# Two residual blocks on one Trainium2 core: the second layer's input finished by an accumulating DMA and ScalarE

## The chip, the cores and the metric

The kernel runs on one core of one Trainium2 chip. The core has a matrix engine (PE, TensorE), a vector engine (DVE, VectorE), an activation engine (ACT, ScalarE), a general engine (POOL, GpSimd) and a queue that mostly issues DMAs (SP, SyncE). They run at the same time and wait for one another by semaphores; each takes its own instructions in order. The metric is the device time of one execution in microseconds: 2819.61 us before the change, the median of three runs (2818.54 to 2820.89).

## The reference, cut to what matters

The input is 64 images of 1024 channels of 14 x 14, in float32. Two bottleneck layers follow one another.

```python
# layer 0: 1x1 to 256, 3x3, 1x1 to 1024; batch statistics over all 64 images
out = relu(_bn(_conv(x, w1, b1), g1, be1))
out = relu(_bn(_conv(out, w2, b2, pad=1), g2, be2))
out = _bn(_conv(out, w3, b3), g3, be3)
y = relu(x + softplus(residual_scale) * out)
# layer 1: deformable; statistics per image and group of channels
a = relu(group_norm(conv(y, w1), ...))
om = conv(a, w_off, pad=1) + b_off          # 27 maps: 9 x offsets, 9 y offsets, 9 masks
sampled = bilinear_sample(a, py, px) * sigmoid(mask)
h2 = relu(group_norm(einsum("bckhw,ock->bohw", sampled, w2), ...))
out = relu(group_norm(conv(h2, w3), ...) + y)
```

Because layer 0's last norm needs statistics over all images, the raw result of its third convolution is written to memory (`h3`) and finished later: `y = relu(scale * h3 + shift + x)`. That last step is what the change is about.

## The kernel before, in words

Two images make a pair, and there are 32 pairs. A pair's activations are tiles of 128 partitions (channels) by 8 blocks by 392 columns (2 x 196 positions).

Layer 0 runs as three loops over all pairs. Products of 2 x 2 blocks are formed with seven instead of eight matmuls, so sums stand before and after the matmuls on DVE, ACT and POOL. Its second convolution leaves even and odd image columns in separate planes. The third convolution (L732 to L863; matmuls at L735, L770, L836) keeps that order in PSUM (`planes`) and stores it to `h3`, one pair after the other. `x` of pairs 0 to 2 is loaded into three of four `Y` buffers during this loop.

Layer 1 runs as one software pipeline over pairs. Pass t, for t from 2 to 29, is written out by hand in `steady(t)` (L1933 to L1974): it lists small steps for PE, and puts steps for the other engines between them at numbered places. On PE, ACT, DVE and POOL the order of the list is the order of the queue. SP's order is left to a planner, except where an instruction is marked to keep its program order. Passes 0, 1, 30 and 31 are made by `slot(t)`, where only PE's order is by hand. In pass t the order on PE is:

- `d1`: the first convolution of pair t+1 (L1109), which reads `y` of pair t+1 (`q["y"]`, one of the four `Y` buffers).
- `sp[0]` woven with the first half of the third convolution `d3` of pair t-1. `sp` samples pair t (L1430, copied out of PSUM by ACT, L1438). In `d3` (L1679), four groups of seven matmuls each need `E` (ACT, L1683), then `V` (DVE, L1686), two sums on POOL (L1691) and two on DVE (L1695, L1699).
- the offset convolution of pair t+1 (`om`, L1205). At its end ACT and DVE form an even and an odd sum (L1220 to L1222), and then six small DVE sums write the offsets (`off`, L1232).
- `sp[1]` woven with the rest of `d3`; at place 7 `selection(t+1)`: ACT's mask (L1244), stores to `dm`, loads of `wt` and `mk`; and there also `load(t+2)`: SP loads `x` into the `Y` buffer (L196) and `h3` into the buffer `Z0` (L204).
- `pd[0]` and `pd[1]`: the second convolution of pair t (L1542), with transposes of pair t+1, the bilinear weights of pair t+1 (`distances`, `end`; L1271 to L1291), the third norm of pair t-1 (a pow on POOL, L1054; scaling on ACT, L1762), and at place 21 of `pd[0]` `residual(t+2)`. In `pd[1]` ACT copies `E` (L1566), DVE forms `V` (L1572), and POOL two sums (L1573, L1574). `output(t-1, 0)` adds `y` (L1778), applies ReLU (L1780) and stores `z` (L1783).

`residual(p)` finishes layer 0 for pair p: for each of the 8 blocks, DVE computes `y = h3 * scale + x`, which also turns the planes of `h3` into image order (L216), and ACT applies shift and ReLU (L228).

Of the kernel before, what the change touches and what calls it, by code (L numbers as in the profile page):

```python
# [16 lines left out]
P = 128  # L17
H = W = 14
HW = H * W
# [25 lines left out]
def kernel(  # L45
# [163 lines left out]
    def end_of_first(p, r, b):  # L209


        def natural(v):
            return v.rearrange("p (r x b) -> p r x b", x=7, b=2)

        y = natural(Y[p % 4][:, b, :])
        return nc.vector.scalar_tensor_tensor(  # L216
            y,

            r[:, b, :].rearrange("p (b r x) -> p r x b", x=7, b=2),
            bn3.sc[:, b : b + 1],  # L220
            y,
            ALU.mult,
            ALU.add,
        )
# [430 lines left out]
    with l0, tc.manual_schedule(  # L655
# [19 lines left out]
        def planes(t):  # L675
            return t.rearrange("p (b n) -> p b n", b=2)

        def relu(p, c, n):
            v = inputs(p, c, n)
            nc.scalar.activation(  # L680
                v, v, AF.Relu, bias=bn2.sh[:, c : c + 1], scale=bn2.sc[:, c : c + 1]
            )
# [49 lines left out]
        for p in range(2):  # L732
            pts = [ps.tile([P, N2], FP, tag=f"ps{o % 4}", name=f"c3_{p}_{o}") for o in range(CB)]
            for o, c in [(o, c) for c in range(MB) for o in range(CB)]:
                nc.tensor.matmul(  # L735
                    planes(pts[o]),
                    w3_sb[:, c, ts(o, P)],
                    inputs(p, c),
                    start=(c == 0),
                    stop=(c == MB - 1),  # L740
                )
            if p == 0:
                for c in range(MB):
                    relu(2, c, 2)
                Ts = input_sums(2)
            else:
                weight_sum(3)
            for o in range(CB):
                d = place(p, o)
                if o % 2:  # L750
                    nc.vector.tensor_scalar(d, pts[o], bias(o), None, ALU.add)
                else:
                    nc.scalar.activation(d, pts[o], AF.Identity, bias=bias(o))
                waiting.append((o, p, d))
                statistics()
            for jj in range(2):
                store_h3(p, jj)
# [5 lines left out]
        for p in range(2, NP - 2, 2):  # L763
            tt = Ts
            for j in range(HB):
                acc = [ps.tile([P, N2], FP, tag=f"ps{m}", name=f"c3_{p}_{j}_{m}") for m in range(4)]
                part = ts(j, P)

                def product(m, a, b, start):
                    nc.tensor.matmul(  # L770
                        planes(acc[m]), a, b, start=start, stop=True, skip_group_check=True
                    )

                e1, e5, e7, u2, w = (
                    ep.tile([P, N2], FP, tag=v, name=f"{v}_{p}_{j}")
                    for v in ("e1", "e5", "e7", "u2", "w")
                )
                (c11, c12), (c21, c22) = ([place(p + i, o) for i in range(2)] for o in (j, HB + j))
                product(0, a11[:, part], inputs(p, 0), True)
                nc.scalar.copy(e1, acc[0])  # L780
                product(1, S[1][:, part], tt[1], True)
                nc.scalar.copy(e5, acc[1])
                product(2, S[3][:, part], tt[3], True)
                nc.scalar.activation(e7, acc[2], AF.Identity, bias=bias(HB + j))
                nc.gpsimd.tensor_tensor(w, e5, e7, ALU.add)
                product(3, S[2][:, part], tt[2], True)

                statistics()
                nc.vector.tensor_tensor(u2, acc[3], e1, ALU.add)
                nc.gpsimd.tensor_tensor(c22, w, u2, ALU.add)  # L790

                product(0, a12[:, part], inputs(p, 1), False)
                nc.scalar.activation(c11, acc[0], AF.Identity, bias=bias(j))
                product(1, S[4][:, part], inputs(p + 1, 1), False)
                nc.vector.scalar_tensor_tensor(c12, acc[1], bias(j), u2, ALU.add, ALU.add)
                product(2, a22[:, part], tt[4], False)
                nc.vector.scalar_tensor_tensor(c21, acc[2], bias(HB + j), u2, ALU.add, ALU.add)
                waiting += [(j, p, c11), (j, p + 1, c12), (HB + j, p, c21), (HB + j, p + 1, c22)]
                if j < 2:
                    relu(p + 2, j, 2)  # L800
                if j == 1 and p in folded:
                    bn3.fold(folded[p], p)
                if j == 2 and p + 2 < NP - 2:
                    Ts = input_sums(p + 2)
                elif j == 2:
                    Ds = [differences(p + 2 + i) for i in range(2)]
                if j % 2:
                    for i in range(2):
                        store_h3(p + i, j // 2)
            if p in (6, 10, 14):  # L810
                load_x((p - 6) // 4)
            elif p == 22:
                load_h3(0, Z0)
            elif p == 26:
                load_h3(1, Z1)

                nc.scalar.activation(small.tile([P, 1], FP, tag="sp_a", name="table"), rs, AF.Sigmoid)
# [8 lines left out]
        for p in range(NP - 2, NP):  # L826
            for o in range(CB):
# [5 lines left out]
                    else ((S[1][:, j], inputs(p, 0)), (a22[:, j], Ds[p - NP + 2]))  # L833
                )
                for m, (a, b) in enumerate(ab):
                    nc.tensor.matmul(planes(pt), a, b, start=(m == 0), stop=(m == 1))  # L836
                d = place(p, o)
                statistics()
                nc.scalar.activation(d, pt, AF.Identity, bias=bias(o))
# [85 lines left out]
    def build_second_bottleneck(l1, path, run, early):  # L925
# [159 lines left out]

        def load(p):
            start(p)

            load_x(p, tc.keep_in_program_order)
            load_h3(p, Z0, tc.keep_in_program_order)  # L1090

        def residual(p, b0=0, b1=CB):

# [93 lines left out]
        def offset_conv(p):  # L1187
# [3 lines left out]
            def step(n):  # L1191
# [20 lines left out]
                if n == 3 * MB - 1:  # L1212


                    om = one.tile([P, N2], FP, tag="om", name=f"om_{p}")[:32]
                    m1, m0, m2, m3 = (
                        q["po"][ts(m, 32)].rearrange("p i q -> p (i q)") for m in range(4)
                    )
                    even, odd = om[:, :HW], om[:, HW:]
                    nc.scalar.activation(even, m1, AF.Identity, bias=boff_sb[:32])  # L1220
                    nc.vector.tensor_tensor(odd, even, m2, ALU.subtract)
                    nc.vector.tensor_tensor(even, even, m2, ALU.add)  # L1222

                    q["om"] = one.tile([32, N2], FP, tag="off", name=f"off_{p}")
                    for h0, h1, _ in groups:
                        dst = q["om"][:, cols(h0, h1)].rearrange("p (i q n) -> p i q n", i=2, n=2)
                        for n, (a, b, op) in enumerate(((even, m0, ALU.add), (odd, m3, ALU.subtract))):
                            a, b = (
                                v.rearrange("p (i q) -> p i q", i=2)[:, :, h0 * half : h1 * half]
                                for v in (a, b)  # L1230
                            )
                            nc.vector.tensor_tensor(dst[:, :, :, n], a, b, op)  # L1232

            return [lambda n=n: step(n) for n in range(3 * MB)]

        def selection(p):

# [1 line left out]

            def step():  # L1240

                om = q["om"]
                mask = one.tile([P, N2], FP, tag="om", name=f"mask_{p}")[:32]
                nc.scalar.activation(mask, om, AF.Sigmoid)  # L1244
# [592 lines left out]
        def slot(t):  # L1837
# [59 lines left out]
            if back and t == NP - 1:  # L1897
                extra.append((32, lambda: output(t - 1, 0)))
            extra += [(20, lambda: first_sum(t, 1))] if this and E == 2 else []
            extra += [(21, lambda: residual(t + 2))] if more else []  # L1900
            extra = [(scale(k), s) for k, s in extra]
            extra.sort(key=lambda v: v[0])
            todo += put(pd[0], [s for _, s in extra], [k for k, _ in extra])
# [12 lines left out]
                extra += list(zip((5, 5, 11), first_norm(2)))  # L1916
            if bare:
                extra.append((n - 6, lambda: corners(t + 1, 0)))
            if back and t < NP - 1:
                extra.append((n * 18 // 28, lambda: output(t - 1, 0)))  # L1920
            elif back:
# [11 lines left out]
        def steady(t):  # L1933
# [9 lines left out]
            def at(steps, *extra):  # L1943
# [5 lines left out]
                ((0,), [lambda: scaled(t - 2, 1)]),  # L1949
                ((1, 1, 7, 9, 9, 10, 10, 10), norm2),  # L1950
                ((6,), [lambda: output(t - 2, 1)]),
                ((10,), [lambda: corners(t, 0)]),
            )
            todo += at(weave(sp[0], d3[:half]), ((4, 4, 8, 14, 16, 18, 21), norm1))
# [1 line left out]
            todo += offset_conv(t + 1)  # L1956
            todo += at(
                weave(sp[1], d3[half + 2 :]),
                ((7, 7), selection(t + 1) + [lambda: load(t + 2)]),
            )  # L1960
            todo += at(
                pd[0],
# [1 line left out]
                ((5, 20), [lambda e=e: first_sum(t, e) for e in range(2)]),  # L1964
                ((6, 11, 16, 21), transposes(t + 1)),
                ((6, 13), [distances, end]),
                ((21,), [lambda: residual(t + 2)]),
            )
            todo += [lambda: list(spread_rows(t + 1, 0)), lambda: list(spread_columns(t + 1, 0))]
            todo += [lambda: list(spread_rows(t + 1, 1)), lambda: lend(t + 1)]  # L1970
            todo += at(pd[1], ((16,), [lambda: output(t - 1, 0)]))
            todo.append(lambda: list(spread_columns(t + 1, 1)))
            for step in todo:
                step()  # L1974
# [200 lines left out]
```

## Time and profile before

| what | value |
|---|---|
| median of the runs | 2819.61 us (2818.54 to 2820.89) |
| the profiled execution | 2822.43 us |
| its span, first to last instruction | 2820.6 us |
| mean granted clock of PE | 0.991 |
| busy in a pass of 56.3 us: PE, DVE, ACT, POOL | 56.14, 48.2, 34.0, 14.4 us |
| DMA, mean over the span | 150 GB/s |

The profile is of one execution, taken by the hardware profiler. Times are in us from the start of the span. A row of the timeline has a start, a duration, the engine, the line, the operation, the tile written and the tiles read, the shape and a count. In square brackets stands how long the engine had been idle before it and what released it. PE shows each float32 matmul as two records. A table by stretches gives each engine's busy time in a part of the span, then the granted clock as a fraction, the mean busy share of the 16 DMA engines, and the GB/s that they moved. Instructions that only issue a DMA do not count as busy.

### The profile page before, as it was taken

How to read it: one execution, taken by the hardware profiler on the slowest of the kernel's cores; microseconds unless marked ns; L12 is line 12 of the kernel's file. 1: busy time of each engine (PE TensorE's matmuls, PEld its weight loads, DVE VectorE, ACT ScalarE, POOL GpSimd, SP SyncE). 2: the span in 40 equal slices, each digit the busy share in tenths (PEclk: the TensorE clock that was granted, in tenths of full speed). 3: DMA queues.
4: the chain of work that ended last, by engine and by line, in shares of the span. 5: the costliest groups of instructions: out<-in, count | busy, mean ns of one | idle time of the engine just before them, and what ended most of it. 6: DMA issues, size and time to landing. Idle time of an engine off the chain costs nothing.

```text
span 2820.6 us, 39474 instructions
## 1 busy us (share of the span) xinstructions
PE 2756.8 (98%) x12930; PEld 2013.2 (71%) x12930; DVE 2376.8 (84%) x4900; ACT 1341.3 (48%) x2723; POOL 951.5 (34%) x1069
## 2 busy tenths in 40 slices
PE   9999899998999989999999999999999999999997
PEld 5555555554555567887888788878887888788874
DVE  7877899998788778888888888888888888888876
ACT  0000221212555545566556655665566556655654
POOL 4630366664666302222222222222222222222221
PEclk9999999999999999999999999999999999999998
DMA  8656000003656444555455545554555455545541
GB/s 233 193 172 175 23 1 0 1 1 132 222 190 227 169 132 146 181 173 189 147 183 175 189 142 182 179 183 146 183 174 190 142 188 172 190 139 190 170 134 58
DMA packets 350315, 424.19 MB, mean 150 GB/s; under 512 B 27892, under 2 KB 292500, under 8 KB 349844
## 3 DMA queue, kind: packets, MB, share of 16 engines
q1 hardware_dynamic: 350100, 421.57, 45.7%
q8 instruction: 104, 1.70, 0.3%
q14 instruction: 111, 0.91, 0.1%
HBM read 296.49 MB, written 116.76 MB: 147 GB/s over the span
## 4 chain that ended last, share of the span: by engine, by line
PE 59%; DVE 2%; issue 1%; DMA 1%; ACT 0%; POOL 0%; SPq 0%; DVEq 0%; ACTq 0%; POOLq 0%
PE pd L1542 22%; PE sp L1430 12%; PE d L1109 11%; PE d L1679 10%; PE om L1205 2%; PE tr L1308 1%; DVE V L1686 1%; PE pd L1461 1%; DMA X<-wd 1%; DMA S<-wd 1%; DVE st L1005 0%; SPq L1393 0%; DVE z L1793 0%; SPq L1349 0%; PE d L1728 0%
## 5 line engine op out<-in xcount | busy, mean ns | idle before, releaser
L1430 PE MATMUL sp<-S,aT 126*128 126x420 f32 (+3 forms) x1536 | 488.3, 416 | 9.1 <-DVE S L1410 7.3
L1438 ACT COPY sm<-sp 128x336 f32<-128x336 f32 (+3 forms) x640 | 288.9, 452 | 257.9 <-PE sp L1430 217.0
L1542 PE MATMUL pd<-sm,w2b_sb 128*128 128x196 f32 x2232 | 400.7, 329 | 0.0
L1542 PEld LDWEIGHTS pd<-sm,w2b_sb 128*128 128x128 f32 x2232 | 371.3, 190 | 0.0
L534 PE MATMUL c<-v,u_sb 128*128 128x392 f32 x1024 | 342.9, 497 | 11.0 <-DVE bn1sh L167 8.2
L1109 PE MATMUL d<-h,w1b_sb 128*128 128x392 f32 x1024 | 345.3, 495 | 2.8 <-ACT h L228 2.8
L534 PEld LDWEIGHTS c<-v,u_sb 128*128 128x128 f32 x1024 | 194.5, 191 | 159.3 <-issue 11.7
L1542 PE MATMUL pd<-sm,Sc 128*128 128x196 f32 x1674 | 308.0, 329 | 0.0
L1109 PEld LDWEIGHTS d<-h,w1b_sb 128*128 128x128 f32 x1024 | 194.0, 191 | 139.5 <-ACT h L228 6.4
L1498 DVE TENSOR_TENSOR sm<-sm 128x980 f32<-128x980 f32 (+2 forms) x257 | 265.8, 1053 | 16.8 <-PE pd L1542 10.1
L1542 PEld LDWEIGHTS pd<-sm,Sc 128*128 128x128 f32 x1674 | 278.7, 190 | 0.2
L1430 PEld LDWEIGHTS sp<-S,aT 126*128 126x128 f32 x1536 | 259.3, 191 | 22.3 <-issue 10.7
L1762 ACT ACTIVATE z<-z,gn_0sh,gn_0sc 128x196 f32<-128x196 f32 x496 | 225.2, 537 | 18.0 <-DVE gn_0sh L1077 18.0
L520 DVE TENSOR_TENSOR v<-t 128x392 f32<-128x392 f32 x256 | 193.0, 812 | 0.0
L1573 POOL TENSOR_TENSOR E<-V,E 128x196 f32<-128x196 f32 x31 | 18.6, 599 | 516.7 <-DVE V L1572 516.7
L1679 PE MATMUL d<-h,w3b_sb 128*128 128x196 f32 x744 | 174.0, 329 | 0.8 <-ACT h L1594 0.8
L1679 PEld LDWEIGHTS d<-h,w3b_sb 128*128 128x128 f32 x744 | 133.6, 189 | 51.6 <-issue 19.1
L1691 POOL TENSOR_TENSOR E<-V,E 128x196 f32<-128x196 f32 x124 | 74.3, 599 | 282.6 <-DVE V L1686 282.6
L1410 DVE TENSOR_TENSOR S<-S,X 126x840 f32<-126x840 f32 (+1 forms) x192 | 159.4, 882 | 11.8 <-DMA X<-wd 10.7
L1780 ACT ACTIVATE z<-z 128x784 f32<-128x784 f32 x124 | 105.8, 857 | 104.3 <-DVE z L1778 102.6
L389 PE MATMUL c<-xc,w1a_sb 128*128 128x392 f32 x384 | 149.1, 497 | 5.6 <-DMA xc<-in_x_dram 5.6
L216 DVE SCALAR_TENSOR_TENSOR h<-h,bn3sc,h 128x392 f32<-128x392 f32 x256 | 140.9, 622 | 0.0
(690 smaller groups left out, 4975.0 us busy)
## 6 DMA issues: line engine op xcount, KB each, us to landing
xc<-in_x_dram SPq DMA_DIRECT2D x128, 392.0 KB
h<-o SPq DMA_DIRECT2D x64, 784.0 KB
h<-in_x_dram SPq DMA_DIRECT2D x64, 784.0 KB
h<-h SPq DMA_DIRECT2D x64, 784.0 KB
out_dram<-z SPq DMA_DIRECT2D x124, 392.0 KB
X<-wd SPq DMA_DIRECT2D x64, 413.4 KB
S<-wd SPq DMA_DIRECT2D x64, 413.4 KB
S<-wd SPq DMA_DIRECT2D x64, 330.8 KB
```

Source lines behind the costliest of these rows:

```text
L216: return nc.vector.scalar_tensor_tensor(y,  r[:, b, :].rearrange("p (b r x) -> p r x b", x=7, b=2), bn3.sc[:, b : b + 1], y, ALU.mult, ALU ...
L389: nc.tensor.matmul(acc[m], a, b, start=(j == 0), stop=(j == HB - 1))
L520: nc.vector.tensor_tensor(v[:, u].rearrange("p (i y x) -> p i y x", y=7, x=7), cols[c][:, :, i : i + 13 : 2, :], cols[c][:, :, j : j + 13 ...
L534: nc.tensor.matmul(m[u], u_sb[:, c, u, k % 4, ts(o, P)], vts[k][c][:, u], start=(c == 0), stop=(c == MB - 1),)
L1109: nc.tensor.matmul(q["pt"][o], w1b_sb[:, c, ts(o, P)], q["y"][:, c, :], start=(c == 0), stop=(c == CB - 1),)
L1410: nc.vector.tensor_tensor(S[:, piece], S[:, piece], X(piece), ALU.mult)
L1430: nc.tensor.matmul(pt[:, i], q["aT"][:, i0 + i, c, starts.index(r0), :], q["S"][e][g, r0][:, :, i0 + i, :], start=(j == 0), stop=(j == len ...
L1438: nc.scalar.copy(dst, pt.rearrange("p i k n -> p k i n"))
L1498: return nc.vector.tensor_tensor(dst, a, b, ALU.subtract)
L1542: nc.tensor.matmul(bank[:, m % 2], a[:, k], b[:, k - k0],  start=(k == 0 and m in (5, 0, 2, 6)), stop=(k == T - 1), skip_group_check=True,)
L1679: nc.tensor.matmul(bank[:, m % 2 if m < 6 else 1], a, b, start=(m < 6), stop=True, skip_group_check=True)
L1762: nc.scalar.activation(z[:, ts(i, HW)], z[:, ts(i, HW)], AF.Identity, bias=n.sh[:, b, i : i + 1], scale=n.sc[:, b, i : i + 1],)
```

## The change

Four things change together.

1. Layer 0's third convolution writes its PSUM tiles in image order (`columns` in place of `planes`: neighbouring outputs lie two words apart within a plane), so `h3` is in image order, and `end_of_first` no longer reorders.
2. In layer 1 `load(p)` loads `h3` straight into the `Y` buffer and no `x`. In `steady` it moves from place 7 of `sp[1]` to place 7 of `d1`.
3. `residual` in the loop is replaced by three steps: `first_scaled` (eight ACT instructions, scale and shift, at place 0 of `pd[0]`), `add_x` (two DMAs issued by POOL that add `x` from memory onto `Y`, at place 12 of `pd[0]`), and `first_relu` (four ACT instructions of two blocks each, at place 0 of `pd[1]`). `slot` gets the same steps at similar places. `residual` remains for pair 2 in the filling of the pipeline.
4. The six offset sums leave the end of `offset_conv` for a step of their own, `offsets`, at place 4 of `sp[1]`, behind the `V` of the running group of `d3`.

```diff
     def end_of_first(p, r, b):
-        def natural(v):
-            return v.rearrange("p (r x b) -> p r x b", x=7, b=2)
-
-        y = natural(Y[p % 4][:, b, :])
+        y = Y[p % 4][:, b, :]
         return nc.vector.scalar_tensor_tensor(
             y,
-            r[:, b, :].rearrange("p (b r x) -> p r x b", x=7, b=2),
+            r[:, b, :],
             bn3.sc[:, b : b + 1],
             y,
             ALU.mult,
             ALU.add,
         )
...
+        def columns(t):
+            return t.rearrange("p (n b) -> p b n", b=2)
...
                 nc.tensor.matmul(
-                    planes(pts[o]),
+                    columns(pts[o]),
...
                     nc.tensor.matmul(
-                        planes(acc[m]), a, b, start=start, stop=True, skip_group_check=True
+                        columns(acc[m]), a, b, start=start, stop=True, skip_group_check=True
...
-                    nc.tensor.matmul(planes(pt), a, b, start=(m == 0), stop=(m == 1))
+                    nc.tensor.matmul(columns(pt), a, b, start=(m == 0), stop=(m == 1))
...
         def load(p):
             start(p)
-            load_x(p, tc.keep_in_program_order)
-            load_h3(p, Z0, tc.keep_in_program_order)
+            load_h3(p, Y[p % 4], tc.keep_in_program_order)
+
+        def first_scaled(p):
+            for b in range(CB):
+                y = Y[p % 4][:, b, :]
+                nc.scalar.activation(
+                    y, y, AF.Identity, bias=bn3.sh[:, b : b + 1], scale=bn3.sc[:, b : b + 1]
+                )
+
+        def add_x(p):
+            for i in range(2):
+                nc.gpsimd.dma_start(
+                    Y[p % 4][:, :, ts(i, HW)],
+                    x[2 * p + i].rearrange("(b p) q -> p b q", p=P),
+                    accum_op=ALU.add,
+                )
+
+        def first_relu(p):
+            for b in range(0, CB, 2):
+                y = Y[p % 4][:, ds(b, 2)]
+                nc.scalar.activation(y, y, AF.Relu)
...
                     om = one.tile([P, N2], FP, tag="om", name=f"om_{p}")[:32]
...
+                    q["sums"] = om[:, :HW], om[:, HW:]
+                    even, odd = q["sums"]
+                    m1, m2 = (q["po"][ts(m, 32)].rearrange("p i q -> p (i q)") for m in (0, 2))
                     nc.scalar.activation(even, m1, AF.Identity, bias=boff_sb[:32])
                     nc.vector.tensor_tensor(odd, even, m2, ALU.subtract)
                     nc.vector.tensor_tensor(even, even, m2, ALU.add)
-                    q["om"] = one.tile([32, N2], FP, tag="off", name=f"off_{p}")
-                    for h0, h1, _ in groups:
...
+        def offsets(p):
+            q = pairs[p]
+            half = W // 2
+            (even, odd), (m0, m3) = q["sums"], (q["po"][ts(m, 32)] for m in (1, 3))
+            q["om"] = one.tile([32, N2], FP, tag="off", name=f"off_{p}")
+            for h0, h1, _ in groups:
+                dst = q["om"][:, cols(h0, h1)].rearrange("p (i q n) -> p i q n", i=2, n=2)
+                for n, (a, b, op) in enumerate(((even, m0, ALU.add), (odd, m3, ALU.subtract))):
+                    a = a.rearrange("p (i q) -> p i q", i=2)
+                    a, b = (v[:, :, h0 * half : h1 * half] for v in (a, b))
+                    nc.vector.tensor_tensor(dst[:, :, :, n], a, b, op)
...
         def selection(p):
             def step():
+                if "om" not in q:
+                    offsets(p)
...
-            extra += [(21, lambda: residual(t + 2))] if more else []
+            extra += [(2, lambda: first_scaled(t + 2)), (12, lambda: add_x(t + 2))] if more else []
...
+            if more:
+                extra.append((n * 8 // 28, lambda: first_relu(t + 2)))
...
                 ((6,), [lambda: output(t - 2, 1)]),
+                ((7,), [lambda: load(t + 2)]),
                 ((10,), [lambda: corners(t, 0)]),
...
                 weave(sp[1], d3[half + 2 :]),
-                ((7, 7), selection(t + 1) + [lambda: load(t + 2)]),
+                ((4, 7), [lambda: offsets(t + 1)] + selection(t + 1)),
...
-                ((21,), [lambda: residual(t + 2)]),
+                ((0, 12), [lambda: first_scaled(t + 2), lambda: add_x(t + 2)]),
...
-            todo += at(pd[1], ((16,), [lambda: output(t - 1, 0)]))
+            todo += at(pd[1], ((0,), [lambda: first_relu(t + 2)]), ((16,), [lambda: output(t - 1, 0)]))
```

More of the change, by code (lines that the diff above doesn't have):

```diff
@@ L1215, in step @@
                     om = one.tile([P, N2], FP, tag="om", name=f"om_{p}")[:32]
[L1216 to L1219, printed above, removed]
+                    q["sums"] = om[:, :HW], om[:, HW:]
+                    even, odd = q["sums"]
+                    m1, m2 = (q["po"][ts(m, 32)].rearrange("p i q -> p (i q)") for m in (0, 2))
                     nc.scalar.activation(even, m1, AF.Identity, bias=boff_sb[:32])
@@ L1222, in step @@
                     nc.vector.tensor_tensor(even, even, m2, ALU.add)
-                    q["om"] = one.tile([32, N2], FP, tag="off", name=f"off_{p}")
-                    for h0, h1, _ in groups:
[L1226 to L1232, printed above, removed]
-            return [lambda n=n: step(n) for n in range(3 * MB)]
+            return [lambda n=n: step(n) for n in range(3 * MB)]
+        def offsets(p):
[9 more added lines that the diff above has]
+                    nc.vector.tensor_tensor(dst[:, :, :, n], a, b, op)
         def selection(p):
```

## The prediction

> **What bounds the kernel.** I read the page first: PE is busy for 98% of the span, DVE for 84%, ACT for 48%. A share of the span is a mean over stages, so next I read busy time in stretches of 56.3 us, the length of one pass of the second layer's loop.
>
> ```profile
> PE 2756.8 (98%) x12930; PEld 2013.2 (71%) x12930; DVE 2376.8 (84%) x4900; ACT 1341.3 (48%) x2723; POOL 951.5 (34%) x1069
> ```
>
> ```profile
> 1771.80:1828.20 56.40, 56.24 (x320) 46.37 (x319) 48.30 (x107) 34.08 (x72) 14.42 (x19) 1.00 0.53 176
> 1828.20:1884.50 56.30, 56.14 (x320) 46.27 (x319) 48.21 (x107) 33.99 (x72) 14.41 (x19) 1.00 0.50 166
> ```
>
> The columns are length, then busy us (and counts) of PE, PEld, DVE, ACT and POOL, then granted clock, DMA share and GB/s. PE is idle for 0.16 us of a pass. All 28 such stretches look alike and make 1577 us of the 2820.6. DVE has 8 us to spare in each. So taking work off DVE is worth nothing here unless a PE wait hangs on it. The timeline of PE in one pass shows the one wait:
>
> ```profile
> 1805.58 0.73 PE L1430 MATMUL sp<-S,aT 126*128 126x336 f32 x2
> 1806.47 0.60 PE L1679 MATMUL d<-T,w3b_sb 128*128 128x196 f32 x2 [0.16 <-DVE V L1686]
> ```
>
> Start to start is 0.89 us, where the same pair without a wait takes 0.57 us (1804.68 to 1805.25): a stall of 0.32 us. DVE's timeline says why: V stands behind the six offset sums.
>
> ```profile
> 1804.43 1.38 DVE L1232 TENSOR_TENSOR off<-om,om 32x84 f32<-32x84 f32 x6
> 1805.85 0.57 DVE L1686 TENSOR_TENSOR V<-d,E 128x392 f32<-128x392 f32 x1
> ...
> 1823.12 4.40 DVE L216 SCALAR_TENSOR_TENSOR h<-h,bn3sc,h 128x392 f32<-128x392 f32 x8
> ```
>
> **Offset sums behind V.** V could start at 1804.43 and end at 1805.0. PE's matmul would then issue at 1806.15, as it would with no wait. The offset sums end 0.57 us later, which delays the mask, the two stores to dm and the loads of wt and mk. Their first reader, L1271 at 1816.76, has some 5 us over, and the loads that followed them on SP's queue are gone from there. Worth 28 x 0.32 = 9.0 us.
>
> **DVE's residual removed.** 8 x 0.55 = 4.40 us per pair leave DVE, worth nothing at a PE without waits.
>
> **ScalarE's new work.** Eight scalings with scale and bias pointers replace nothing at the start of `pd[0]`, T0 = 1812.40 here. L228 (one pointer, 392 wide) costs 4.22 us for eight; L1762 (two pointers, 196 wide) shows 0.08 us more of fixed cost each, so I take 0.61 us x 8 = 5.0 us: from 1812.7, after the last sm copy, to 1817.7. ACT has the room:
>
> ```profile
> 1814.80 0.37 ACT L1311 COPY aT<-tr 126x256 f32<-126x256 f32 x1 [2.10 <-PE tr L1308]
> 1817.76 0.86 ACT L1272 ACTIVATE wt<-wt 126x784 f32<-126x784 f32 x1 [2.58 <-DVE wt L1271]
> ...
> 1824.03 4.22 ACT L228 ACTIVATE h<-h,bn3sh 128x392 f32<-128x392 f32 x8
> 1830.45 0.49 ACT L1566 COPY E<-pd 128x392 f32<-128x392 f32 x1 [2.20 <-PE pd L1542]
> ```
>
> The aT copy slips by 2.9 us (its PSUM buffer is wanted again only by the fourth transpose at 1820.02) and Abs by 0.3 us (the next DVE step runs at 1820.67 anyway). Four ReLUs of 784 at 0.87 us (row L1780, 0.86) then stand where L228 stood: 3.5 us for 4.2. Without lateness this costs nothing; with the cover gone it would be 5.0 us a pair.
>
> **The load moved.** Two h3 loads (L204, 784 KB each) go from behind the selection to step 7 of `d1`, two x loads (L196) leave SP. On SP they follow the spreads of X and the stores of z at 1785.6, and SP has nothing behind them until 1805.8. They wait for the z+y sum that ends at 1784.1. They stand behind the stores in one queue, so do not slow them. At the 350 to 410 GB/s of the loads below they need 4.3 us, and land by 1799; the reader comes at 1812.7. Nothing.
>
> **The accumulating DMA** is what decides. It sits on POOL behind the pow of 1815.84 to 1817.4, waits for the last scaling (1817.7), and moves 2 x 802,816 B in rows of 784 B. Behind it on POOL stand the E and h2 sums at 1833.76, 16 us later. The ReLUs wait for it; behind these on ACT stands E (L1566), behind E comes V (L1572 at 1833.12), then h2, its norm, and PE's third convolution; and the first convolution, at 1834.17, reads the ReLUs' output. Where is the deadline? If both transfers land at time L, E ends at L + 4.0 instead of 1830.94. V then starts at L + 4.0 instead of 1833.12, and in the next pass the T sums on POOL are ready some 2 us ahead of the matmuls that read them (1787.41 against 1789.42). So L up to about 1831.2 is free, and each us later costs one us of PE. The first convolution's own limit is 1834.17 - 0.9 = 1833.3, less strict.
>
> When does it land? The DMA engines, in the same pass (share and GB/s are the last columns):
>
> ```profile
> 1814.00:1816.00 2.00, 2.00 (x15) 1.98 (x14) 1.79 (x8) 0.37 (x1) 0.16 (x1) 1.00 1.11 353
> 1816.00:1818.00 2.00, 2.00 (x15) 1.97 (x14) 2.00 (x3) 0.24 (x1) 1.40 (x1) 1.00 1.11 400
> 1822.00:1824.00 2.00, 2.00 (x14) 2.00 (x13) 2.00 (x4) 2.00 (x7) 0.00 (x0) 1.00 0.36 99
> 1826.00:1828.00 2.00, 2.00 (x14) 2.00 (x13) 2.00 (x4) 2.00 (x5) 0.00 (x0) 1.00 0.53 186
> 1830.00:1832.00 2.00, 2.00 (x14) 2.00 (x13) 2.00 (x3) 1.20 (x2) 0.00 (x0) 1.00 0.57 224
> 1832.00:1834.00 2.00, 2.00 (x14) 2.00 (x13) 0.99 (x3) 1.97 (x5) 0.24 (x1) 1.00 0.70 228
> ```
>
> A plain pair load runs at about 378 GB/s with the engines full: 1.61 MB in 4.25 us. No row shows an accumulate. Its bounds: once that price, and three times or more. The Trainium skill, DMA: Bandwidth & Descriptors, section Anatomy of one DMA, fits a POOL-issued DMA as 2.0 us plus bytes over 436 GB/s. By it both are down 5.7 us after 1817.7, at 1823.4: in time. The same page's Rules for kernel authors speak against that: an accumulate reads its destination before it writes it. Two streams read for one written make 8.5 us of full engines, an estimate from the page and the row. I take this, since the plain rate is already that of full engines. From 1819 (1.3 us to begin, an estimate from the page's first-byte figure), some 0.7 of the engines is free until 1822 (the stores of wd alone, estimated) and 0.64 and 0.74 in the next two stretches: 4.9 us of engine time by 1826; of the other 3.6 us half-shares bring the end to 1833.2, and leftovers alone to 1835.5. With 1 us to complete, L is 1834.2 to 1836.5: 3.0 to 5.3 us late. I take 3.6, nearer the even share.
>
> A second rule, SBUF — State Buffer, section SBUF: two separate sides, says that DVE in a two-port mode keeps POOL from writing descriptors. In 1817.7 to 1821 DVE runs almost only tensor_tensor, which by the same page has no such mode. Followed blindly it would add the DVE rows in that stretch, 3 us a pair (87 us); I add nothing.
>
> **First layer in image order.** Matmul outputs go to PSUM at a step of two words (L735, L770, L836: 64 + 784 + 64 records of 0.329 us pitch, 300 us). No row shows a strided PE write: between 0 and +300 us, and I take 0, since a column already takes 0.84 ns. The 16 residual instructions of the first two pairs lose their stride: at most 16 x 0.06 = 1 us. Taken as 0.
>
> **Sum.** The profiled execution took 2822.4 us (span 2820.6). Minus 9.0, plus 29 pairs (3 to 31) x 3.6 = 104: 2917.8. The median of the runs is 2.8 us below the profiled time: 2915.
>
> **The rivals.** *In time, faster:* the accumulate costs less than about 1.6 plain loads (6.8 us of engines), L stays under 1831.2, ACT never blocks, only the 9.0 us remain: 2811 (2803 to 2816). For it: the pass's DMA share of 0.53 and the page's fit. Against: the second read. *Far late:* at three prices or with slow descriptors on POOL, 12.8 us of engines end near 1843: 13 us x 29 = 377 us, about 3190. The stores of z then slip too: they drain by about 1793, just when POOL rewrites z (1793.47). And stalls of 3 us or more lower the clock:
>
> ```profile
> 1018.00:1020.00 2.00, 0.38 (x4) 0.17 (x2) 0.00 (x0) 0.00 (x0) 0.00 (x0) 1.00 0.58 219
> 1020.00:1022.00 2.00, 0.66 (x1) 0.50 (x2) 1.80 (x4) 0.25 (x1) 0.00 (x0) 0.64 0.59 217
> 1022.00:1024.00 2.00, 2.00 (x4) 0.94 (x3) 2.00 (x6) 1.34 (x4) 0.00 (x0) 0.50 0.60 232
> ```
>
> After 3 us of idle PE runs at half clock for 5.4 us, 2.7 us lost; 29 times would be 78 us. *Strided writes slow:* up to 3100 alone.
>
> **Chances.** A few us late 0.42 (own range 2850 to 2985); in time 0.31; far late 0.22; strided writes or another cause 0.05. A measurement tells some 0.2% (5.6 us) from no change: of the in-time case 0.04 falls within it, and 0.03 of the late case where lateness just eats the 9 us. So faster 0.27, same 0.07, slower 0.66. The range must hold the in-time case below and stops where 0.17 of far late and strided writes is left above, at 2.35 plain prices (7 us a pair, with some lost clock): 2804 to 3045.
>
> **What would show it.** V's wait gone and L1686 ahead of the offset sums: the 9 us right. ACT idle before the 784-wide ReLUs, released by a DMA later than 19 us after T0, and PE idle before L1109 or L1679: the late case, with the idle time as its size. No such idle, and a pass of 56.0 us: in time. Longer L770 durations: the strided write. I would be wrong if the accumulate runs at the plain rate, or if it runs with so little overlap that a row at a time pays its full latency.

## The result: 2888 us, 2.4% slower

The changed kernel takes 2888.36 us (median of four runs, 2886.1 to 2889.72) where the kernel before takes 2820.23 in the same session: a ratio of 1.0242 [1.0224, 1.0259]. The profiled execution has a span of 2884.0 us against 2820.6, at a granted clock of 0.992.

First the page of the changed kernel: busy time, the two large DMA queues (packets, MB, share of 16 engines' span), the chain that ended last, and the adding DMA (KB each, median us from issue to landing).

```profile
PE 2782.8 (96%) x12930; PEld 2015.4 (70%) x12930; DVE 2254.8 (78%) x4668; ACT 1428.9 (50%) x2839; POOL 1044.8 (36%) x1127
...
q1 hardware_dynamic: 289780, 375.01, 40.8%
q0 software_dynamic: 60320, 46.57, 11.5%
...
PE 32%; DMA 14%; DVE 7%; ACT 7%; issue 3%; SPq 2%; POOL 1%; DVEq 0%; ACTq 0%; POOLq 0%
...
h<-in_x_dram POOLq DMA_DIRECT2D x58, 784.0 KB, 10.6
```

The same chain of the kernel before:

```profile
PE 59%; DVE 2%; issue 1%; DMA 1%; ACT 0%; POOL 0%; SPq 0%; DVEq 0%; ACTq 0%; POOLq 0%
```

DVE lost 122 us of work, about as forecast, and PE still lost time. The chain was 59% PE before; now a DMA holds 14% of it. The queue q0 carries only the adding DMAs: 46.57 MB in 60320 packets, 772 B each. Its 11.5% of 2884.0 us are 332 us, or 11.4 us over 16 engines for each of 29 pairs. (It is a sum of packet times. Stretches below add up to more than 1, so it isn't an occupancy; it serves to compare kernels.) Two stretches of one pass's length show where PE stands (columns as in the prediction):

```profile
1861.50:1920.00 58.50, 57.29 (x320) 46.51 (x319) 44.05 (x98) 37.28 (x77) 17.61 (x21) 1.00 0.65 167
1920.00:1978.50 58.50, 57.33 (x320) 46.44 (x320) 44.08 (x99) 37.36 (x77) 17.64 (x21) 1.00 0.63 167
```

The same 320 matmuls need 58.5 us. PE is idle for 1.2 of them instead of 0.16; its busy time is 1.2 us longer too, since a pair of matmuls behind a wait is longer in the records (0.60 us for L1702 in the timeline below, 0.50 without a wait). So idle time alone shows half of the loss. I measure passes from the start of one offset convolution to that of the next: 56.33 us before, 58.41 after, mean of 27 passes.

The chain of waits (us in all, times, longest us; PEld is PE's weight load):

```profile
ACT h L1109 <- DMA h<-in_x_dram: 250.8, 29, 9.7
...
DVE V L1595 <- ACT E L1589: 137.2, 29, 7.0
...
PEld d L1702 <- ACT h L1617: 40.8, 31, 4.1
PEld sp L1453 <- DVE S L1433: 26.4, 30, 2.3
PEld d L1702 <- DVE z L1718: 20.0, 30, 1.0
...
PE d L1702 <- ACT h L1617: 21.6, 30, 3.5
...
PE sp L1453 <- DVE S L1433: 19.0, 31, 2.0
```

Read down, it is one path: the ReLUs wait for the adding DMA, `V` for `E` behind the ReLUs, PE's third convolution for the second norm's ReLU (L1617), its sampling matmuls for `S`, a product on DVE, and later in the pass the third convolution's weight loads for DVE's sum `z` (L1718). The timeline of one pass, with T0 = 1896.40, has the places (rows of DVE, ACT, POOL, PE and SP put together in order of time):

```profile
1888.77 0.57 DVE L1709 TENSOR_TENSOR V<-d,E 128x392 f32<-128x392 f32 x1
1889.36 1.38 DVE L1255 TENSOR_TENSOR off<-om,om 32x84 f32<-32x84 f32 x6
...
1896.60 4.95 ACT L1094 ACTIVATE h<-h,bn3sh,bn3sc 128x392 f32<-128x392 f32 x8
1901.91 3.19 POOL L1100 DMA_DIRECT2D h<-in_x_dram  x2 [0.50 <-ACT aT L1334]
1903.54 4.26 SPq L1314 DMA_DIRECT2D wd<-wt  x4
1913.67 2.44 SPq L1372 DMA_DIRECT2D S<-wd  x3
1916.80 3.10 ACT L1109 ACTIVATE h<-h 128x784 f32<-128x784 f32 x4 [8.66 <-DMA h<-in_x_dram]
1919.81 0.46 ACT L1589 COPY E<-pd 128x392 f32<-128x392 f32 x1
1920.30 0.57 DVE L1595 TENSOR_TENSOR V<-pd,E 128x392 f32<-128x392 f32 x1 [4.48 <-ACT E L1589]
1929.41 0.60 PE L1702 MATMUL d<-h,w3b_sb 128*128 128x196 f32 x2 [0.54 <-ACT h L1617]
1930.51 0.97 PE L1453 MATMUL sp<-S,aT 126*128 126x420 f32 x2 [0.49 <-DVE S L1433]
```

The first two rows are the offset sums behind `V`: that part does what it says. The ReLUs start at T0+20.4, ACT having stood for 8.66 us, and `V` at T0+23.9 where it was at T0+20.72: 3.18 us late. The first convolution, which begins at T0+21.78 in both kernels, isn't held up. PE pays after it, at the third convolution. The engines' share during the adding DMAs (last two columns):

```profile
1904.00:1906.00 2.00, 2.00 (x15) 1.98 (x14) 2.00 (x3) 2.00 (x6) 1.11 (x1) 1.00 0.97 111
1906.00:1908.00 2.00, 2.00 (x14) 2.00 (x13) 1.21 (x2) 2.00 (x7) 0.00 (x0) 1.00 1.23 201
1908.00:1910.00 2.00, 2.00 (x14) 2.00 (x13) 0.00 (x0) 0.14 (x1) 0.00 (x0) 1.00 1.27 181
1914.00:1916.00 2.00, 2.00 (x14) 2.00 (x13) 1.82 (x3) 0.00 (x0) 0.00 (x0) 1.00 1.02 162
```

Full engines, at half the GB/s that the plain loads of before reached with full engines (353 and 400).

### The profile page after: what moved, and what is told of

The parts are those of the page before. It is cut to its first block, busy times and chain, and to the rows that moved or that the text cites. A ratio compares the mean times of both kernels' runs of the same rounds, so it can differ in the third digit from the quotient of the medians.

```text
span 2884.0 us, 39588 instructions
## 1 busy us (share of the span) xinstructions
PE 2782.8 (96%) x12930; PEld 2015.4 (70%) x12930; DVE 2254.8 (78%) x4668; ACT 1428.9 (50%) x2839; POOL 1044.8 (36%) x1127
## 3 DMA queue, kind: packets, MB, share of 16 engines
q0 software_dynamic: 60320, 46.57, 11.5%
## 4 chain that ended last, share of the span: by engine, by line
PE 32%; DMA 14%; DVE 7%; ACT 7%; issue 3%; SPq 2%; POOL 1%; DVEq 0%; ACTq 0%; POOLq 0%
PE sp L1453 13%; PE d L1702 10%; DMA h<-in_x_dram 9%; PE pd L1565 6%; ACT h L1094 3%; PE om L1224 2%; DMA S<-wd 2%; DMA X<-wd 2%; ACT h L1109 2%; DVE st L1006 1%; DVE z L1801 1%; DVE S L1433 1%; DMA wd<-wt 1%; SPq L1372 1%; DMA out_dram<-z 1%
## 5 line engine op out<-in xcount | busy, mean ns | idle before, releaser
L1461 ACT COPY sm<-sp 128x336 f32<-128x336 f32 (+3 forms) x640 | 283.0, 453 | 245.2 <-PE sp L1453 212.7
L530 PEld LDWEIGHTS c<-v,u_sb 128*128 128x128 f32 x1024 | 194.7, 191 | 158.7 <-DVE v L516 11.5
L1109 ACT ACTIVATE h<-h 128x784 f32<-128x784 f32 x116 | 89.8, 844 | 250.8 <-DMA h<-in_x_dram 250.8
L1702 PE MATMUL d<-h,w3b_sb 128*128 128x196 f32 x744 | 177.2, 334 | 21.6 <-ACT h L1617 21.6
L1702 PEld LDWEIGHTS d<-h,w3b_sb 128*128 128x128 f32 x744 | 131.4, 189 | 82.4 <-ACT h L1617 40.8
L1094 ACT ACTIVATE h<-h,bn3sh,bn3sc 128x392 f32<-128x392 f32 x232 | 143.8, 705 | 2.5 <-DMA h<-h 2.5
## 6 DMA issues: line engine op xcount, KB each, us to landing
h<-in_x_dram POOLq DMA_DIRECT2D x58, 784.0 KB, 10.6
```

The lines of the kernel that those rows point to most:

```text
L530: nc.tensor.matmul(m[u], u_sb[:, c, u, k % 4, ts(o, P)], vts[k][c][:, u], start=(c == 0), stop=(c == MB - 1),)
L1094: nc.scalar.activation(y, y, AF.Identity, bias=bn3.sh[:, b : b + 1], scale=bn3.sc[:, b : b + 1])
L1461: nc.scalar.copy(dst, pt.rearrange("p i k n -> p k i n"))
L1702: nc.tensor.matmul(bank[:, m % 2 if m < 6 else 1], a, b, start=(m < 6), stop=True, skip_group_check=True)
```

## The experiments

**Theory A**: the landing comes later than ACT's order can bear, and each microsecond past a deadline is a microsecond of the pass. **Theory B**: the adding DMA crowds out other transfers, and their lateness is what costs. Later I add what the adding costs in itself. Where an expectation numbers its theories otherwise, its own words hold.

### The offset sums alone

```diff
 # the kernel before, with only the offset sums as a step of their own
-                ((7, 7), selection(t + 1) + [lambda: load(t + 2)]),
+                ((4, 7, 7), [lambda: offsets(t + 1)] + selection(t + 1) + [lambda: load(t + 2)]),
```

> The kernel before with the offset sums alone moved behind V (place 4 of sp[1]); nothing else of the change. If the stall of 0.32 us (0.42 with the slower restart after it) is what the offset sums cost, 28 passes lose 9 to 12 us: 2808 to 2811 us, a pass of 55.9 to 56.0 us and no wait of PE on V. If the order of DVE only shifts the stall to a later sum, 2820 us.

2810.73 us against 2819.32, ratio 0.9971 [0.9960, 0.9983]. Passes go from 56.33 to 56.00 us. This is the fastest kernel of all: the change holds a gain of 8.6 us and a loss of 77.6 us (2888.36 - 2810.73). The two spans are 75.1 us apart: 27 passes x 2.41 = 65.2, the last pass 5.5, pass 1 another 4.2 (67.46 against 63.22 us), together 74.9.

### Plain copies in place of the accumulate

```diff
                     x[2 * p + i].rearrange("(b p) q -> p b q", p=P),
-                    accum_op=ALU.add,
```

> The changed kernel with plain copies in place of the accumulating ones: same queue (POOL), same bytes, same waits; the addition of x is left out, each copy overwrites the scaled result. If the accumulate itself (its second read) makes the transfer late, the engines need about a third to a half of the time, both land at least 4 us earlier, ACT stops waiting for them or nearly so, and the time is 2809 to 2816 us. If a DMA issued by POOL is late as such (descriptors, queue), it stays above 2870 us.

2814.86 us, ratio 0.9986 [0.9979, 0.9993]. The ReLUs start at T0+13.4 (median) and all written-out passes take 56.00 us. A stretch during these copies moves about twice what a stretch of the adding DMA moves:

```profile
1818.00:1820.00 2.00, 2.00 (x15) 2.00 (x13) 2.00 (x3) 2.00 (x6) 0.00 (x0) 1.00 1.05 353
```

ACT's scalings, POOL's issue, the moved load and the image order are all still there, so they cost nothing in a steady pass; of the 77.6 us, 73.5 hang on the word "accumulate". The 4.1 us that remain over the offset sums alone sit in pass 1 (68.25 us against 63.22).

### The ReLUs behind E on ACT

```diff
-            todo += at(pd[1], ((0,), [lambda: first_relu(t + 2)]), ((16,), [lambda: output(t - 1, 0)]))
+            todo += at(pd[1], ((17,), [lambda: first_relu(t + 2)]), ((16,), [lambda: output(t - 1, 0)]))
```

> The changed kernel with the four ReLUs at place 17 of pd[1] instead of 0 in the 28 hand-written passes, behind ACT's copy of E and the ReLUs of z. Theory A, ACT is blocked in order by the wait and so E, V and h2 come 3.2 us late: E is on time again, the first convolution's limit is 21 us after the start of pd[0] against a landing at 20.3, and the time falls to 2808 to 2822 us. Theory B, the crowded DMA engines delay the spreads and the stores of z by 5 to 6 us and that is what PE waits for: nothing changes, 2880 us or more. Both: in between.

2820.41 us, ratio 1.0006 [0.9997, 1.0014]: 68 us of the 77.6 come back, though the adding DMAs are the same and land no earlier (the second of a pair at T0+20.3 in the median, T0+20.4 in the changed kernel). What is left of the waits:

```profile
POOL z L1714 <- DMA out_dram<-z: 32.6, 26, 2.2
...
DVE z L1718 <- DMA out_dram<-z: 14.4, 17, 2.0
...
ACT h L1109 <- DMA h<-in_x_dram: 10.5, 15, 3.9
```

ACT's wait for the DMA fell from 250.8 to 10.5 us. In its place POOL and DVE wait for stores of `z`, which leave late. Theory B is there, but small: 5.5 us over the plain copies in the medians. Theory A is the loss.

### One image of the two accumulated

```diff
-                    accum_op=ALU.add,
+                    **({"accum_op": ALU.add} if i == 0 else {}),
```

> The changed kernel where only the first image of a pair is accumulated and the second is copied plainly, so its addition of x is left out. Theory A with a limit near 18.8 us after the start of pd[0]: the landing comes 2 to 3 us earlier (17 to 18 us), inside the limit, and nearly all is won back: 2810 to 2820 us. If every us of accumulate costs PE in proportion (theory B), half of the loss stays: 2845 to 2855 us.

2825.1 us, ratio 1.0028 [1.0018, 1.0039]: 63 us of the 77.6 come back, 5 us short of the range expected under theory A. ReLUs at T0+18.1, passes of 56.32 us in the mean (median 56.05). ACT still waits 177.0 us for the DMA and little of it costs: here the landing stands just at the deadline. Which reader sets that deadline can be seen here, too: the waits for L1617 and for `S` are back to 4.5 and 4.1 us in the whole run, and one of the three is left:

```profile
PEld d L1702 <- DVE z L1718: 13.8, 24, 1.4
```

### The adding DMAs issued later

```diff
         def add_x(p):
+            for _ in range(5):      # two in the second run
+                nc.gpsimd.tensor_tensor(delay, delay, delay, ALU.add)
```

> The changed kernel with five extra sums of 128x196 on POOL (0.6 us each on a scratch tile) in front of each pair of accumulating DMAs, so that these start 2 to 3 us later. Theory A: past the limit each us later costs one us of PE, so a pass grows by 2 to 3 us and the time by 58 to 87 us: 2945 to 2975 us. If only the crowding of the DMA engines counted, a later start would move the crowding, and the time would change by less than 30 us.

3109.66 us, ratio 1.1025 [1.1006, 1.1043], at a clock of 0.960: 221 us more than the changed kernel, far outside what I expected.

> As the changed kernel, with two (not five) extra sums of 128x196 on POOL ahead of the two adding DMAs of each pair; the sums go to a tile that nobody reads. From the five-sum kernel: one extra sum takes 0.95 us on POOL, and five moved the issue of the DMAs by 4.15 us and the ReLUs by 8.4 us, so the ReLUs moved twice as far as the issue. Two should move the issue by 1.4 us and the ReLUs by 2 to 3 us, from T0+20.3 to T0+22.3 to 23.3. Theory A (a deadline for the ReLUs at about T0+17.8 through ACT's order, and one us of the pass for each us past it, up to the point where the next step, the first convolution, waits as well): a pass of 60.5 to 61.5 us, 29 x (2.0 to 3.0) = 58 to 87 us over the changed kernel, 2946 to 2975 us, PE's clock above 0.98. Theory C (what cost 221 us with five sums is mostly a step, such as lost clock, that begins somewhere past the changed kernel's lateness): either next to nothing over what the lateness alone gives, or a clock under 0.975 and over 2985 us.

2909.88 us (two runs), ratio 1.032 [1.029, 1.035], clock 0.991: 21.5 us more, this time below what I expected. Beside one another the runs make a line. ReLU is the median start of the ReLUs from T0; the loss is the mean pass over the 56.00 us of the plain copies.

| kernel | first adding DMA issued | ReLU | mean pass | loss | ReLU - loss |
|---|---|---|---|---|---|
| plain copies | T0+5.4 | 13.4 | 56.00 | 0 | |
| half accumulated | T0+5.5 | 18.1 | 56.32 | 0.3 | 17.8 |
| changed kernel | T0+5.5 | 20.5 | 58.41 | 2.4 | 18.0 |
| two sums ahead | T0+7.1 | 21.3 | 59.32 | 3.3 | 17.9 |
| five sums ahead | T0+9.7 | 28.7 | 66.62 | 10.6 | 18.1 |

The deadline is T0+18.0 within 0.2, and past it each us costs one. Single passes say the same: over the 27 passes of the changed kernel the ReLUs start between T0+20.0 and T0+21.4, and start less loss, as in the last column, stays between 17.8 and 18.4 (18.2 in the mean); with two sums the starts reach T0+24.4 and the mean is 18.2 again.

Both expectations failed at another point: how far a later issue moves the landing. Issued 1.5 us later it came 0.8 later; issued 4.2 us later it came 8.3 later. The timelines of SP suggest a reason, which no run tests by itself. With two sums the loads of `S` leave at about T0+16.5, when the first of the two adding DMAs has landed (they leave at T0+17.3 in the changed kernel, T0+11.15 before). With five sums two of the four stores of `wd` are out well before the adding DMAs, so the loads of `S` and `X` leave from T0+12.5 to 13.0 on, when neither has landed, and run beside both. Then PE runs dry long enough for its clock. The stretches of one such pass:

```profile
1896.00:1898.00 2.00, 2.00 (x14) 2.00 (x13) 0.93 (x2) 0.00 (x0) 0.00 (x0) 1.00 1.20 263
1898.00:1900.00 2.00, 1.45 (x9) 1.15 (x7) 0.00 (x0) 0.00 (x0) 0.00 (x0) 1.00 0.73 152
1900.00:1902.00 2.00, 0.00 (x0) 0.00 (x0) 0.00 (x0) 0.00 (x0) 0.00 (x0) 1.00 0.65 176
1902.00:1904.00 2.00, 0.00 (x0) 0.00 (x0) 0.00 (x0) 0.00 (x0) 0.00 (x0) 1.00 0.67 237
1904.00:1906.00 2.00, 0.77 (x1) 0.50 (x2) 0.00 (x0) 1.68 (x3) 0.00 (x0) 0.63 0.63 224
1906.00:1908.00 2.00, 2.00 (x4) 1.01 (x3) 0.19 (x1) 2.00 (x4) 0.00 (x0) 0.50 0.64 222
```

PE is idle for 5.77 us and then works at 0.50; the 32 matmuls of the first convolution take 13.82 us where they took 10.70. That makes 8.9 of this pass's 9.7 us, and these stretches are the far-late rival as the prediction drew it. So the row of five sums stands on the line partly by chance: its loss comes by another way, the wait in front of the first convolution (188.8 us in 27 waits) and the half clock behind it.

### Long rows

```diff
-                    Y[p % 4][:, :, ts(i, HW)],
-                    x[2 * p + i].rearrange("(b p) q -> p b q", p=P),
+                    Y[p % 4][:, ts(i, HB)].rearrange("p b q -> p (b q)"),
+                    h3[p][:, ts(i, HB * N2)],
                     accum_op=ALU.add,
```

> The changed kernel where the accumulating DMAs read h3 (rows of 6272 bytes) in place of x (rows of 784 bytes); same bytes, queue and waits. The addition of x is left out, h3 is added again instead. If an accumulate costs by its bytes (each read twice), the share of the software queue stays near 11.5% and the time near 2888 us. If its price is that of short rows, one packet each, the share falls towards the 5.3% of the plain copies, the wait of ACT falls under 2 us a pair, and the time to 2810 to 2825 us.

2817.59 us, ratio 0.9995 [0.9988, 1.0002]; passes of 56.06 us. The queue and the issue of this kernel:

```profile
q0 software_dynamic: 8352, 46.57, 8.7%
...
h<-h POOLq DMA_DIRECT2D x58, 784.0 KB, 8.5
```

and of the plain copies:

```profile
q0 software_dynamic: 11136, 46.57, 5.3%
...
h<-in_x_dram POOLq DMA_DIRECT2D x58, 784.0 KB, 6.8
```

Per pair, the share times the span over 29: plain copies 5.1 us over 16 engines, accumulate in rows of 6272 B 8.5, accumulate in rows of 784 B 11.4. Of the 6.3 us that the accumulate adds, 2.9 go with the short rows and 3.4 stay with rows eight times as long. The plain copies move the very rows of 784 B, yet in packets of 4182 B (46.57 MB by 11136); accumulating, the same rows are packets of 772 B. So the share fits neither branch of the expectation: it falls by about half of what separates the two. Its two DMAs cover four blocks each, so the first two ReLUs wait for the first only and start at T0+11.9; but the second DMA, too, lands at T0+16.1 (median), inside the deadline. POOL's issue of a pair is short again as well, here beside that of the plain copies:

```profile
1818.62 1.82 POOL L1100 DMA_DIRECT2D h<-h  x2
```

```profile
1814.78 1.82 POOL L1100 DMA_DIRECT2D h<-in_x_dram  x2 [0.44 <-ACT aT L1333]
```

### The load of pass 1

```diff
 # with the ReLUs behind E
-            loads = [lambda: load(t + 2)] if t + 2 < NP and not (early and t < 1) else []
+            loads = [lambda: load(t + 2)] if t + 2 < NP and not (early and t < 2) else []
+            if early and t == 1:
+                load(3)
```

> The changed kernel with the late ReLUs (place 17 of pd[1]) and with the h3 load of pair 3 moved from behind the selection to the start of pass 1. If the 4 to 7 us that pass 1 loses come from ACT waiting for that load with E behind it, they are won back: 2812 to 2815 us, and the offset convolution of pass 1 to that of pass 2 takes 63 us again in place of 70. If the planner's new order of pass 1 costs them, it stays at 2820 us. The remainder over 2811 us would be the stores of z.

2818.01 us, ratio 0.9994 [0.9987, 1.0001]. This asks for the 4.2 us of pass 1. With the ReLUs behind `E` and the load where the change has it, that pass shows on ACT and on PE:

```profile
1076.17 0.71 ACT L1094 ACTIVATE h<-h,bn3sh,bn3sc 128x392 f32<-128x392 f32 x1 [4.29 <-DMA h<-h]
...
1077.91 1.02 PE L1702 MATMUL d<-T,w3b_sb 128*128 128x196 f32 x2 [4.18 <-DVE V L1709]
```

A scaling waits for `h3` to be loaded, `E` and `V` stand behind it, and PE waits for them. With the load at the start of the pass the longest wait of PE there is 0.57 us and the pass takes 65.45 us instead of 70.17. Against the kernel before, though, the medians moved by only 1.8 us (from 1.1 over it to 0.7 under it), where I had expected 5 to 8. The profiled execution with the late load was 4.4 us above its own median, so its pass of 70.17 us may be longer than usual. The stall and its cause are shown; what it is worth in the whole is not settled.

### The changed kernel with the offset sums back in front of V

```diff
                     nc.vector.tensor_tensor(even, even, m2, ALU.add)
+                    offsets(p)
...
-                ((4, 7), [lambda: offsets(t + 1)] + selection(t + 1)),
+                ((7,), selection(t + 1)),
```

> The changed kernel with the offset sums put back in front of V. If the two effects add, the stall of V comes back: 28 x 0.33 = 9 us more, 2895 to 2900 us. If the late pass hides it, because PE waits there anyway, 2888 us.

2894.46 us, ratio 1.0264 [1.0247, 1.0281]: 6.1 us over the changed kernel, just under the range expected; passes 58.72 against 58.41. Beside the late DMA the offset sums are worth 0.31 us a pass, alone 0.33: the two effects add.

## Why the prediction was right where it was, and where it wasn't

The likeliest case, "a few us late", is what happened, at 2888 where 2915 was named. The way of the loss was forecast; its size came out of errors that in part cancel. By its steps:

- **Offset sums, 9.0 us.** Right: 8.6 alone, 0.33 us a pass where 0.32 was read from two start times.
- **DVE's residual, nothing.** Right: 122 us of DVE left and no pass is shorter for it.
- **ScalarE's scalings, 5.0 us and no cost.** Right: 4.95 us, and passes of 56.00 us with plain copies.
- **The load moved, nothing.** Right for the written-out passes, where no scaling waits. Wrong for pass 1, which the step left out: its ACT order comes from the planner, and the scalings stand ahead of `E` before `h3` is there. By the length of that pass its term was about 4 us.
- **The accumulating DMA, 3.6 us x 29 = 104.** The mechanism was right: the ReLUs' wait, `E` behind them, `V`, the third convolution, one us for each us. The size was half as large again as it should have been: 2.4 us a pass in 27 passes. There are errors both ways in it.
  - *Engine time*, taken as 8.5 us for two reads: 11.4. Long rows took just these 8.5, but that is partly luck: a plain copy from POOL took 5.1 and not 4.25, and the accumulate 1.7 times that and not twice. The short packets came on top. The Trainium skill's fit for a POOL-issued DMA (DMA: Bandwidth & Descriptors, section Anatomy of one DMA), the basis of the in-time reckoning, comes out too short beside this pass's other traffic: from the last scaling on it had both transfers down by T0+11, and even plain copies let the ReLUs start only at T0+13.4.
  - *Landing*, taken as T0+21.8 to 24.1: T0+20.5, earlier in spite of the larger price. I had given the adding DMA what others leave free, then half shares. It didn't take leftovers: shares stayed at 1.0 to 1.27, and it was SP's issue of the stores of `wd` that stretched from 2.52 to 4.26 us and the loads of `S` that left 6 us later. (The bound from leftovers alone was also summed too early: the rows from 1826 to 1836 leave 3.4 us of the 3.6, so it ends after 1836 and not at 1835.5.)
  - *Deadline*, taken as T0+18.8: T0+18.0. From ReLU start to `V` are 3.5 us, not 4.0, which leaves `V` in place up to T0+17.2; but the cushion behind it isn't the 2 us of POOL's T sums. It is 0.8 us by the runs, and the reader that has so little is DVE's sum `z` further on in the same pass, for which the third convolution's weight loads wait: this wait is what is left in the half-accumulated kernel, at the deadline. In the kernel before, the sum ended at 1794.87, 0.65 us ahead of the load:

```profile
1794.30 0.57 DVE L1695 TENSOR_TENSOR z<-d,E 128x392 f32<-128x392 f32 x1
1795.52 0.19 PEld L1679 LDWEIGHTS d<-T,Sb 128*128 128x128 f32 x1 [0.17 <-issue]
```

- **POOL's descriptors, nothing.** Right as far as the runs go. Issuing a pair of adding DMAs holds POOL for 3.2 us against 1.8 for plain copies of the same shape in the same place, but 1.8 again for an accumulate in long rows. So what lengthens it goes with the short rows of the accumulate, and neither with the adding as such nor with DVE's work beside it. What a quieter DVE would do wasn't tried.
- **Strided PSUM writes, 0 of at most 300 us.** Right. The largest group of the third convolution's largest line, of before and after (durations in ns: shortest, median, longest; then the first and last start in us):

```profile
L770 PE MATMUL c<-h,w3a_sb x336: 492/492/493, 688.2 to 944.6; 128*128 128x392 f32 x168
```

```profile
L771 PE MATMUL c<-h,w3a_sb x336: 492/492/493, 686.9 to 943.3; 128*128 128x392 f32 x168
```

The ends of matmuls are modelled in a profile, so the starts count more: from the first to the last are 256.4 us in both. The residual's instructions that lose their stride are 24, not the 16 counted; they show no loss either (0.61 us each in the mean, 0.62 before).

- **The clock.** It held at 0.992, as assumed for a few us late. The half clock of the far-late case came with 5.8 us of idle PE, in the kernel with five sums. The prediction read it too short: at the stall that it shows, the clocks of the four stretches from 1020 to 1028 (0.64, 0.50, 0.50, 0.66) add up to 6.8 us at half, not 5.4.
- **Stores of z**, which I had put in the far-late case alone: they slip already here, and are the likely part of the 5.5 us that remain once the ReLUs have moved; no run took them away by themselves.

## What to carry to other kernels

Before a wait is put on an in-order engine, work out the latest moment at which it may end: the instruction queued behind it, that one's reader, and so on to the engine that sets the time, with the narrowest cushion on that way. When a wait can't end in time, moving the waiting instruction behind the urgent one can be worth nearly as much as a faster transfer: one place number won back 68 of the 78 us here, where long rows won back 71 and plain copies 74, both without the sum that the kernel needs. Price an accumulating DMA by its rows: in rows of 784 B its packets took 2.2 times the time of the plain copy's, in rows of 6272 B 1.7 times.

## What the hardware showed that I had not expected

- Accumulating splits what a plain copy joins: with the same 784-B rows 2080 packets a pair of 772 B against 384 of 4182 B, and 3.2 us against 1.8 us of POOL to issue them; in rows of 6272 B it is 288 packets and 1.8 us.
- The mean busy share of the 16 engines, a sum of packet times, isn't a share of a fixed budget: with the adding DMA on it stood at 1.02 to 1.27 for 10 us, at 160 to 200 GB/s; with plain copies it was 1.05 at 353 GB/s.
- A delay can grow or shrink on its way through shared DMA engines: 1.5 us at the issue were 0.8 us at the landing, 4.2 us were 8.3. What else had left before is the likely reason, not a tested one.
